# Two fused layers on one core: another order for layer 1's block maxima

## The chip, the cores and the metric

One core of one Trainium2 chip runs the whole program; there is one launch and no other core takes part. The metric is device time of that core in microseconds (us), the median of the runs shown. TensorE (PE in the profile, with its weight loads as PEld), VectorE (DVE), ScalarE (ACT), GpSimd (POOL) and the DMA queue of SyncE (SP) each work through their own list of instructions in order and meet at semaphores.

## The reference, cut to what matters

The input has 4 batches of 2048 rows of 256 numbers. Layer 0 is a gated recurrence plus an attention over 4 chosen heads. Layer 1, where the change lies, is a causal attention with 16 heads of 16 numbers plus a channel mix. All is in float32.

```python
def _L1_attn_ref(x, W_q, b_q, W_k, b_k, W_v, b_v, W_o, b_o):
    ...
    scores = jnp.einsum('bhid,bhjd->bhij', Qh, Kh) / jnp.sqrt(jnp.asarray(Dh, dtype=x.dtype))
    causal = jnp.tril(jnp.ones((S, S), dtype=x.dtype))
    scores = scores * causal - NEG_BIG * (1.0 - causal)
    attn = jax.nn.softmax(scores, axis=-1)
    vals = jnp.einsum('bhij,bhjd->bhid', attn, Vh)
    ...
    return vals @ W_o + b_o
...
x = x + _L1_attn_ref(xn, ...) + _L1_ffn_ref(xn, ...)
```

The softmax needs, for each query and head, the largest score over the keys that the mask leaves.

## The kernel before

**Groups, blocks, units.** Layer 1 takes its 16 heads in 4 groups `g` of 4. The 4 heads of a group lie in four strips of 32 partitions, so that four matmuls with 32 rows each can run side by side. Queries and keys are cut into 4 blocks of 512 (`q` for queries, `kc` for keys) and each block into 4 tiles of 128 rows (`t`).

**Maxima.** A `Maxima(q, t, kc)` unit computes the scores of one tile of 128 queries against one block of keys for the four heads: four matmuls (L767), each into one PSUM bank, and a VectorE reduction of each. A unit with `kc < q` is full: 512 columns, reduced by a plain TENSOR_REDUCE (L773). A unit with `kc == q` lies on the diagonal and is masked: it has only (t + 1) * 128 columns, and its reduction (L770) adds the mask. Block `q` has 4(q + 1) units, four of them masked, with 128, 256, 384 and 512 columns. When all units of a block are done, `turn` reduces and transposes the maxima (L832, L835) and sends them by four DMAs on SP into a spare row of the query tile. From then on the maximum is subtracted by the score matmul itself.

**Weights.** A `Weights(q, t)` unit takes one tile of 128 keys against a block of 512 queries: four matmuls (L792), four exponentials on ScalarE (L794), for the four diagonal tiles a mask on GpSimd (L797), later four matmuls with the values (`weigh`, L803), a copy out of PSUM by ScalarE (L809) and an addition on GpSimd (L810). Its width is 512, or on the diagonal 512, 384, 256 and 128 in turn. Block `q` has 4q + 4 of these, so a group has 40 units of each kind.

**How they are paired.** The loop of `layer1` makes one step of one Weights unit `w` and one Maxima unit `m`, and `Leading` runs the maxima 20 units ahead of the weights (the first 20 of a batch are done while layer 0's attention ends and layer 1 opens):

```python
for h in range(0, 4, 2):
    w.scores(h)
    w.scores(h + 1)
    if m is not None:
        m.scores(2 - h)
        m.scores(3 - h)
if before is not None:
    weigh(before)
```

A step so issues eight score matmuls in two rounds of four, two strips for `w` and two for `m`, and then the four value matmuls of the step before. Each takes the next of the 8 PSUM banks (`own_bank`): nine banks are asked for per step, so a bank comes round again in the next step and must have been emptied by then. Everything is issued in program order on each engine (`in_order`).

Steps are numbered 0 to 39 in a group here. The Maxima unit in step n is the 20th after: steps 4 to 19 carry block 3 of the same group, steps 20 to 23 block 0 of the next group, 24 to 31 block 1, 32 to 39 and the 0 to 3 that follow block 2. In the last group of a batch no maxima are left from step 20 on.

Of the kernel before, what the change touches and what calls it, by code (L numbers as in the profile page):

```python
# [18 lines left out]
P = 128  # L19
QB = 512  # L20
EPS = 1e-5
MASKED = -1e30


# [48 lines left out]
def two_layers(ctx: ExitStack, tc: tile.TileContext, x, Wa, Wx, ba, bx, Lam,  # L73
# [8 lines left out]
    NT = T // P  # L82
    NQ = T // QB
    NH, NA, DH = 16, 4, 64
    NG, DH1 = 4, 16
    SC0 = 1.0 / math.sqrt(DH)
    LN8 = math.log(8.0)
# [40 lines left out]
    def rows_of(both, n, count):  # L128
# [13 lines left out]
    POOL.memset(cmask, 0.0)  # L142
    POOL.affine_select(out=cmask[:, QB - P:QB], in_=cmask[:, QB - P:QB], compare_op=ALU.is_ge, fill=MASKED,
                       base=0, pattern=[[-1, P]], channel_multiplier=1)
    eps_c = const.tile([P, 1], FP, tag="eps", name="eps_c")
    POOL.memset(eps_c, EPS)
    quarter_c = const.tile([P, 1], FP, tag="quarter", name="quarter_c")
# [607 lines left out]
    class Maxima:  # L755
# [9 lines left out]
        def scores(self, h):  # L765
# [3 lines left out]
            if self.own:  # L769
                DVE.tensor_tensor_reduce(out=s[:, 0:n], in0=s[:, 0:n], in1=cmask[:, QB - n:QB], scale=1.0,  # L770
                                         scalar=2 * MASKED, op0=ALU.add, op1=ALU.max, accum_out=self.mx[:, h, :])
            else:
# [39 lines left out]
    class Leading:  # L812
# [6 lines left out]
        def all(self):  # L819
            for g in range(NG):  # L820
                for q in range(NQ):
                    mx = sm.tile([P, 4, 4, q + 1], FP, tag="mx1", name=f"mx1_{self.b}_{g}_{q}",
                                 padded_shape=[P, 4, 4, NQ])
                    for t in range(4):
                        for kc in range(q + 1):
                            yield Maxima(q, t, kc, *self.qk[g], mx)
                    self.turn(g, q, mx)

        def turn(self, g, q, mx):
# [272 lines left out]
```

## Time and profile before

| What | Before |
|---|---|
| Median of 3 runs | 4263.85 us (4263.78 to 4267.86) |
| Profiled execution, its own time | 4265.95 us |
| Span of that execution | 4264.2 us |
| Mean granted TensorE clock | 0.995 |
| PE busy | 4155.7 us (97%) |
| DVE busy | 3103.7 us (73%) |
| ACT busy | 2809.0 us (66%) |
| POOL busy | 1044.7 us (25%) |
| L767, matmuls of the maxima | 1138.7 us busy, 5120 of them |
| L773, reductions of full units | 951.7 us busy, 1536 of them |
| L770, reductions of masked units | 473.2 us busy, 1024 of them |
| L792, score matmuls of the weights | 1075.4 us busy, 5120 of them |

Each of the 4 batches runs through the same stages in the same order; layer 1's loop is the stretch from 593 to 1084 us in the first of them. Busy time counts an instruction from its start to its end, also where several of one engine overlap, so a PE that is busy need not be working at its full rate.

### The profile page before, as it was taken

The page shows a single profiled execution, that of the slowest core. Times are in us where ns is not written, and L with a number is a line of the kernel's source. Part 1 is how long each engine was busy: PE and PEld are TensorE (multiplying, and loading weights), DVE is VectorE, ACT ScalarE, POOL GpSimd, SP SyncE. Part 2 cuts the span into 40 slices and gives each one's busy share as a digit, 9 for nine tenths or more (in the row PEclk, how much of TensorE's full clock was granted, in tenths as well). Part 3 has the DMA queues.
Part 4 walks back from the last instruction along what each step waited for, and adds up shares of the span by engine and source line. Part 5 has one row for each costly group of instructions (what it writes and reads, how often), then busy time and mean ns, then how long its engine had stood idle before and what let it go on. Part 6 is the DMA issues. An engine that isn't in the chain of part 4 may idle for free.

```text
span 4264.2 us, 86371 instructions
## 1 busy us (share of the span) xinstructions
PE 4155.7 (97%) x32994; PEld 2300.1 (54%) x32994; DVE 3103.7 (73%) x7292; ACT 2809.0 (66%) x6388; POOL 1044.7 (25%) x1322
## 2 busy tenths in 40 slices
PE   6999999999999999999999999999999999999998
PEld 3777643334477764333457776433446777643334
DVE  5777678887577767888757776788856767688882
ACT  3666648886566655888656665588865666568884
POOL 0000015544100002654410000255440000036544
PEclk9999999999999999999999999999999999999999
DMA  3000010100100001110000000011000000101000
GB/s 86 1 11 1 6 19 16 18 26 17 27 1 11 1 6 19 17 37 6 19 24 1 11 1 9 16 17 37 7 19 23 1 11 1 21 6 17 16 7 23
DMA packets 70818, 65.79 MB, mean 15 GB/s; under 512 B 37234, under 2 KB 58628, under 8 KB 68868
## 3 DMA queue, kind: packets, MB, share of 16 engines
q1 hardware_dynamic: 66624, 57.19, 6.1%
q8 instruction: 260, 4.26, 0.4%
q10 hardware_dynamic: 3780, 3.07, 0.2%
q14 instruction: 154, 1.26, 0.1%
HBM read 16.70 MB, written 8.39 MB: 6 GB/s over the span
## 4 chain that ended last, share of the span: by engine, by line
PE 89%; DVE 5%; ACT 3%; issue 1%; POOL 1%; DMA 1%; ACTq 0%; SPq 0%; POOLq 0%; DVEq 0%
PE bank L792 15%; PE bank L767 13%; PE bank L803 12%; PE bank L515 10%; PE bank L493 10%; PE bank L540 10%; PE bank L989 4%; PE bank L698 3%; PE bank L289 3%; PE bank L553 2%; DVE mx L773 1%; PE bank L472 1%; PE bank L455 1%; PE bank L977 1%; DVE mx L497 1%
## 5 line engine op out<-in xcount | busy, mean ns | idle before, releaser
L794 ACT ACTIVATE p<-bank 128x512 f32<-128x512 f32 (+3 forms) x2560 | 1183.3, 540 | 299.7 <-PE bank L792 194.9
L767 PE MATMUL bank<-k,q 32*128 32x512 f32 (+3 forms) x5120 | 1138.7, 569 | 1.7
L773 DVE TENSOR_REDUCE mx<-bank 128x1 f32<-128x512 f32 x1536 | 951.7, 682 | 238.1 <-PE bank L767 235.1
L792 PE MATMUL bank<-q,k 32*128 32x512 f32 (+3 forms) x5120 | 1075.4, 557 | 0.0
L507 ACT ACTIVATE p<-bank,nm 128x512 f32<-128x512 f32 x1024 | 689.5, 685 | 568.1 <-DVE nm L501 568.0
L810 POOL TENSOR_TENSOR o<-o,w 128x512 f32<-128x512 f32 (+3 forms) x576 | 627.3, 1089 | 796.6 <-ACT w L809 795.0
L792 PEld LDWEIGHTS bank<-q,k 32*128 32x128 f32 x5120 | 422.9, 184 | 547.1 <-ACT p L794 407.0
L497 DVE TENSOR_REDUCE mx<-bank 128x1 f32<-128x512 f32 x1024 | 645.8, 683 | 93.7 <-PE bank L493 93.1
L803 PE MATMUL bank<-p,v 128*17 128x512 f32 (+3 forms) x5120 | 602.9, 535 | 21.7 <-ACT p L794 14.3
L521 DVE COPY pT<-bank 128x512 f32<-128x512 f32 x512 | 352.7, 691 | 294.1 <-PE bank L515 277.9
L770 DVE CUSTOM_DVE_ANT_0 bank<-bank,cmask 128x128 f32<-128x128 f32 (+3 forms) x1024 | 473.2, 522 | 111.5 <-PE bank L767 56.3
L540 PEld LDWEIGHTS bank<-pT,v 128*64 128x64 f32 x8192 | 441.9, 137 | 193.2 <-issue 193.2
L493 PE MATMUL bank<-k,q 64*128 64x512 f32 x2048 | 542.8, 610 | 1.1 <-ACT p L507 0.3
L515 PE MATMUL bank<-ident,p 128*128 128x128 f32 x4096 | 492.1, 275 | 19.9 <-ACT p L507 19.7
L540 PE MATMUL bank<-pT,v 128*64 128x128 f32 x8192 | 503.7, 276 | 0.0
L767 PEld LDWEIGHTS bank<-k,q 32*128 32x128 f32 x5120 | 430.8, 184 | 129.5 <-DVE mx L773 42.4
L515 PEld LDWEIGHTS bank<-ident,p 128*128 128x128 f32 x4096 | 445.3, 141 | 71.1 <-ACT p L507 29.4
L706 POOL MEMSET q<- 128x2048 f32 x16 | 28.9, 1805 | 1655.1 <-PE bank L540 1655.1
L809 ACT COPY w<-bank 128x512 f32<-128x512 f32 (+3 forms) x576 | 305.4, 530 | 107.8 <-PE bank L803 85.2
L521 ACT COPY pT<-bank 128x512 f32<-128x512 f32 x512 | 293.4, 600 | 61.6 <-PE bank L515 59.7
L803 PEld LDWEIGHTS bank<-p,v 128*17 128x17 f32 x5120 | 88.8, 95 | 441.0 <-ACT p L794 236.6
L493 PEld LDWEIGHTS bank<-k,q 64*128 64x128 f32 x2048 | 211.5, 188 | 171.1 <-issue 84.3
(164 smaller groups left out, 3350.6 us busy)
## 6 DMA issues: line engine op xcount, KB each, us to landing
x<-in_L_attn_x_dram SPq DMA_DIRECT2D x20, 512.0 KB
q<-q SPq DMA_DIRECT2D x64, 128.0 KB
vals<-o SPq DMA_DIRECT2D x256, 32.0 KB
out_dram<-x SPq DMA_DIRECT2D x32, 256.0 KB
q<-qp SPq DMA_DIRECT2D x48, 128.0 KB
k<-kp SPq DMA_DIRECT2D x48, 128.0 KB
q<-nmT SPq DMA_DIRECT2D x256, 2.0 KB
q<-qp SPq DMA_DIRECT2D x64, 32.0 KB
```

What stands on the lines that cost most here:

```text
L493: PE.matmul(self.s[j][i], lhsT=self.qT[i][half_, self.t * P:(self.t + 1) * P], rhs=self.kT[half_, j * QB:(j + 1) * QB], start=True, stop=True)
L497: DVE.tensor_reduce(self.mx[:, n:n + 1], self.s[j][i], AX.X, ALU.max)
L507: ACT.activation(self.p[j][:, i, :], self.s[j][i], AF.Exp, bias=nm, accum_out=self.sums[:, n:n + 1])
L515: PE.transpose(self.tr[j][i][:, n * P:(n + 1) * P], self.p[j][:, i, n * P:(n + 1) * P], ident)
L521: copy(self.pT[:, n0:n0 + 4, :], self.tr[j][i].rearrange("p (n q) -> p n q", q=P))
L540: PE.matmul(acc[i * DH:(i + 1) * DH, 0:P], lhsT=self.v[h][:, N * j + n, self.k * DH:(self.k + 1) * DH], rhs=tile_.pT[:, 8 * h + N * j + n, ...
L767: PE.matmul(s[:, 0:n], lhsT=self.qT[strip(h), self.qs], rhs=self.kT[strip(h), self.ks], start=True, stop=True)
L773: DVE.tensor_reduce(self.mx[:, h, :], s[:, 0:n], AX.X, ALU.max)
L792: PE.matmul(s[:, c0:QB], lhsT=self.kT[strip(h), self.ks], rhs=self.qT[strip(h), self.q0 + c0:self.q0 + QB], start=True, stop=True)
L794: ACT.activation(p[:, h % 2, c0:QB], s[:, c0:QB], AF.Exp, scale=SC1)
L803: PE.matmul(acc[32 * h:32 * h + DH1 + 1, c0:QB], lhsT=self.v[h], rhs=self.p[h // 2][:, h % 2, c0:QB], start=True, stop=True)
L810: POOL.tensor_tensor(self.o[:, c0:QB], self.o[:, c0:QB], w[:, c0:QB], ALU.add)
```

## The change

The order of the Maxima units within a block is read from a table. An entry is a tile digit and a key block digit: "23" is tile 2 against key block 3. The units of a block, their matmuls and reductions, the tile of maxima they write and the moment of `turn` stay what they are.

```diff
+MAXIMA = ("30 20 10 00", "30 11 10 00 20 21 31 01", "31 30 20 11 22 21 12 10 00 32 01 02",
+          "02 23 31 21 00 30 03 13 12 33 32 22 10 01 11 20")
...
+    assert NQ == len(MAXIMA)
...
-                    for t in range(4):
-                        for kc in range(q + 1):
-                            yield Maxima(q, t, kc, *self.qk[g], mx)
+                    for unit in MAXIMA[q].split():
+                        yield Maxima(q, int(unit[0]), int(unit[1]), *self.qk[g], mx)
```

The pairs that result in the steps of a group, with the width of the Weights unit, and for the Maxima unit f for a full one and the number of columns for a masked one:

```
steps     weights           maxima before                    maxima after
0 to 3    512 384 256 128   384 f f 512                      f 512 f 128
4 to 7    512 (all)         f f f 128                        f 384 f f
8 to 11   512 384 256 128   f f f 256                        f f 128 256
12 to 19  512 (all)         f f f 384 f f f 512              f 512 f f f f f f
20 to 23  512 384 256 128   128 256 384 512                  512 384 256 128
24 to 31  512 (all)         f 128 f 256 f 384 f 512          f 256 f f f 384 512 128
32 to 35  512 (all)         f f 128 f                        f f f f
36 to 39  512 384 256 128   f 256 f f                        384 f 256 f
```

## The prediction

> **What bounds the kernel now.** I read the page first, then the timeline of one group, then busy time by stretches of its steps.
>
> ```profile
> PE 4155.7 (97%) x32994; PEld 2300.1 (54%) x32994; DVE 3103.7 (73%) x7292; ACT 2809.0 (66%) x6388; POOL 1044.7 (25%) x1322
> ...
> PE 89%; DVE 5%; ACT 3%; issue 1%; POOL 1%; DMA 1%; ACTq 0%; SPq 0%; POOLq 0%; DVEq 0%
> ```
>
> By the engine totals and the chain of waits PE is the bound, and the change takes no work from it. Whether it works at its full rate must be seen in the steps. Two steps with a full unit on both sides, third group of the first batch:
>
> ```profile
> 869.19 0.19 PEld L792 LDWEIGHTS bank<-q,k 32*128 32x128 f32 x2 [0.85 <-ACT p L794]
> ...
> 869.48 0.62 ACT L809 COPY w<-bank 128x512 f32<-128x512 f32 x1
> ...
> 870.35 2.06 ACT L794 ACTIVATE p<-bank 128x512 f32<-128x512 f32 x4 [0.25 <-PE bank L767]
> 870.43 2.48 DVE L773 TENSOR_REDUCE mx<-bank 128x1 f32<-128x512 f32 x4 [0.62 <-PE bank L767]
> ...
> 871.20 1.05 PE L803 MATMUL bank<-p,v 128*17 128x512 f32 x8
> ```
>
> A step runs from one such L792 load to the next. Most full steps take 2.91 us: two rounds of scores and one of values, 0.97 us each (1.9 ns a column). This one takes 3.00, because it follows a masked unit. ACT needs 2.06 + 0.62, DVE 2.4 (four reductions, one every 0.60 to 0.62 us). So PE is full only where both units are full. Where `w` is 512 wide and `m` is masked with 128 to 384 columns, the step falls only to 2.79 (ACT's), and the next full one takes 3.00: a short `m` beside a full `w` saves 0.03 us. Next, the same group by steps 0-5, 6-7, 8-13, 14-19, 20-24, 25-35, 36-39:
>
> ```profile
> 824.22:841.20 16.98, 16.96 (x149) 7.32 (x145) 15.75 (x37) 12.26 (x30) 8.24 (x14) 1.00 0.10 17
> 841.20:846.90 5.70, 5.38 (x53) 2.08 (x49) 4.64 (x15) 4.76 (x10) 4.25 (x3) 1.00 0.40 72
> 846.90:863.48 16.58, 16.48 (x148) 6.63 (x144) 13.67 (x28) 13.22 (x31) 8.94 (x14) 1.00 0.74 170
> 863.48:881.15 17.67, 17.65 (x148) 6.37 (x144) 14.19 (x30) 15.27 (x30) 6.34 (x5) 1.00 0.04 9
> 881.15:894.28 13.13, 12.97 (x124) 6.12 (x121) 10.35 (x42) 10.23 (x26) 8.51 (x13) 1.00 0.01 3
> 894.28:926.45 32.17, 31.60 (x269) 11.75 (x265) 24.57 (x68) 28.21 (x56) 11.88 (x10) 1.00 0.03 6
> 926.45:937.24 10.79, 10.78 (x100) 4.38 (x96) 8.84 (x21) 8.13 (x21) 7.83 (x12) 1.00 0.01 2
> ```
>
> Columns: length, then busy PE, PEld, DVE, ACT, POOL. PE shows busy throughout, yet its columns in these 113.0 us (3 x 17408 x 1.9 ns) are 99 us. The 14 us between are lost where widths don't match; two such places:
>
> ```profile
> 856.47 0.30 PEld L767 LDWEIGHTS bank<-k,q 32*128 32x128 f32 x4 [0.29 <-DVE mx L773]
> ...
> 884.97 0.43 DVE L770 CUSTOM_DVE_ANT_0 bank<-bank,cmask 128x256 f32<-128x256 f32 x1 [1.30 <-PE bank L792]
> ```
>
> In step 11 (`w` 128) PE waits for a bank that VectorE, late from the full unit in step 10 (`w` 256), has not emptied. In step 21 VectorE stands idle 1.30 us, since its units are short while `w` is long; in step 23 (`w` 128, `m` 512) it is the last instead.
>
> **The change part by part.** It adds and removes nothing: same matmuls, reductions, DMAs, each in its old place in its engine's list, with another width. `turn` with its SP DMAs comes after the same unit count, and the steps between it and its first reader stay four or more (about 9 us against 2.5 us for its DMAs). What moves is which widths meet. Per group, masked units beside a 512 `w` go from 10 to 8, and beside narrow ones the small `m` now meets the small `w`.
>
> For each step I take the largest of: PE, (w + m + w of the step before) x 1.9 ns; DVE, four reductions at 0.60 us full, and 0.65, 0.51, 0.38, 0.25 masked by width (spacing in the timeline), plus 0.65 for `turn`; ACT, 2.79 for a 512 `w` behind another, else four exponentials (2.06 at 512, 0.89 at 128) and the copy (0.60 to 0.30); POOL, 0.82 for the diagonal mask and 1.27, 1.00, 0.72 or 0.45 for the addition. The ratio of measured to this sum is carried over.
>
> Steps 20 to 24. Before 2.79 + 2.18 + 2.06 + 2.60 + 3.05 = 12.68, measured 13.13 (x1.035). After 2.91 + 2.43 + 1.82 + 1.54 + 2.51 = 11.21 (PE, PE, POOL, POOL, DVE; step 23 leaves VectorE room for part of `turn`), x1.035 = 11.60. Gain 1.5.
>
> Steps 36 to 39 and 0 to 5. Before 2.91 + 2.18 + 2.40 + 2.40 + 2.36 + 2.67 + 2.40 + 2.60 + 3.05 + 2.91 = 25.88, measured 10.79 + 16.98 = 27.77 (x1.073). After 2.79 + 2.67 + 1.82 + 2.40 + 2.40 + 2.67 + 2.40 + 1.54 + 2.51 + 2.79 = 23.99, x1.073 = 25.74: gain 2.0. I take 1.7, as in short steps the delay from a matmul to the freed bank weighs more.
>
> Steps 8 to 13. Before 2.91 + 2.67 + 2.40 + 1.54 + 2.40 + 2.91 = 14.83, measured 16.58. After, step 10 falls to 1.82 (POOL): ratio alone gives 0.65. Following the banks by hand (VectorE no longer late in step 11) gives 1.2. I take 0.9. In the second group POOL also adds a bias in each of these steps (L923, 0.73 us): 0.3 there.
>
> Costs. Full units moved beside a 512 `w`: 0.1 a group. In the last group the mix makes VectorE the bound in steps 14 to 17 (4.98 us busy of 5.00 in the stretch 987 to 992), and step 15 gets a full unit for a 384: 0.4 a batch. In the 20 leading units, 256 more columns (0.43 us of PE, 1.1 of DVE), and the first unit is 512 wide, not 128: its VectorE work of 2.6 us, not 1.0, stands ahead of two copies of layer 0's attention (L521). VectorE idled 4.44 us before it, and the four units' sum is the same. Nothing to 3.8 us; I take 1.2.
>
> Per batch: 3 x 1.5 + 3 x 1.7 + 0.5 (the first group's own steps 0 to 5, half covered by layer 1's opening) + 3 x 0.9 + 0.3 - 4 x 0.1 - 0.4 - 1.2 = 11.1. Four batches: 44 us. The profiled execution took 4265.95 us, 1.75 outside its span, and is 2.1 above the median; the change lies within the span, so I take it off the median: 4263.85 - 44.4 = 4219.5.
>
> **Two rules against the trace.** The row PE 97% says that at most 3% is to be had; taken as the bound, the group could give 113.02 - 111.82 = 1.2 us, 14 to 16 us in all. The Trainium skill, "Perfetto Trace Analysis", Identifying the Most-Contended Engine, says that matmul busy time is a bad measure because matmuls are pipelined, and to look at weight loads: 54% here. I follow it, and the 99 us of columns with it. Against the change speaks "TensorEngine Tiling (Array Packing)", PSUM Bottleneck: tiling speeds up TensorE but not the emptying of PSUM, which may then bind. As a rule for totals it gives no gain, since DVE and ACT empty the same columns as before. The rows say DVE 92.0 and ACT 92.1 of 113.0 us: neither is full over a group, but each is last in some steps, and that is what the pairing changes. I go by the rows, and keep the rule for the rivals.
>
> **The rivals.** (a) GpSimd takes over in the short steps. Its mask and addition are in order, and `weigh` waits for the mask. If steps 3, 10, 22, 23, 38 stay near 2.3 us (step 11 now: 2.23), steps 20 to 24 gain 0.5, 36 to 5 gain 1.0, 8 to 13 0.4: 1.5 + 3.0 + 0.3 + 1.4 - 2.0 = 4.2 a batch, 17 us, 4247. For: 8.51 us busy of 13.13 in steps 20 to 24. Against: 4.6 us of room.
> (b) No change: the narrow steps gain 3 to 6 a batch, little more than in (a), and the lead takes its full 3.8, so that the costs are 4.6: 4258 to 4270. For: the two copies that VectorE makes late feed layer 0's last value matmuls. Against: its 4.44 us of idle time just before.
> (c) Slower. A wide pair makes VectorE late, and the step behind it pays at the bank ring: step 1 now takes 3.17 where its PE sum is 2.67. If step 21 behind the new 512 pair takes 3.17 and 22 and 23 stay at 2.44 and 2.36, 20 to 24 is 2.91 + 3.17 + 2.44 + 2.36 + 2.97 = 13.85, 0.7 more; 36 to 5 lose 0.2, 8 to 13 gain 0.2: 2.1 + 0.6 - 0.8 + 2.0 = 3.9 a batch, 4279. It decides if step 21 takes over 3 us and step 23 stays over 2.2. Against: step 22 and 23 need less of VectorE than they last, so lateness dies out there.
> (d) That the change doesn't do what it says: it does not keep masked units apart (block 0 has only such, block 1 ends with three in a row). My sum does not rest on that.
>
> **How the numbers follow.** My forecast 0.64 (4198 to 4240; the lower end has the hand-followed gains of 1.75, 2.0 and 1.2 and no costs, 65 us); (a) 0.18; (b) 0.09; (c) 0.09. About 0.2%, 8.5 us, is what a measurement of this kernel tells from no change. Faster (below 4255.3) 0.82: forecast and (a); same 0.09: (b); slower 0.09: (c). The range, 4197 to 4258, takes in (a) and ends where (b) begins.
>
> **What would show it.** Right: per group, steps 20 to 24 near 11.6 us, 36 to 5 near 26, 8 to 13 near 15.6, steps 24 to 35 unchanged, the waits of L767 for L773 and L770 (42.4 and 19.6 us) smaller, granted clock still 0.995. POOL: L803 waiting for L797 grows from 38.4 us. Wrong: step 21 over 3 us or 23 over 2.2; a lead of more than 61.86 + 2 us from the first L767 to the first L792; or 24 to 35 longer by over 0.5.

## The result, and the profile after

| What | Before | After |
|---|---|---|
| Median | 4264.70 us (the three runs of before and one more) | 4233.02 us (4 runs, 4232.47 to 4234.65) |
| Ratio, 95% interval | | 0.9926 (0.9910 to 0.9941) |
| Span of the profiled execution | 4264.2 us | 4232.9 us |

The changed kernel is 31.7 us faster: 0.74%, with an interval of 0.6 to 0.9%. The forecast was 44 us. Line numbers after the change are 5 higher around the loop (L767 is now L772, L792 is L797, L803 is L808) and 4 higher further down; in experiments that add a line they are one higher still.

The page of the changed kernel, the engine totals and the chain of waits by engine:

```profile
PE 4129.7 (98%) x32994; PEld 2283.5 (54%) x32994; DVE 3107.5 (73%) x7292; ACT 2797.4 (66%) x6388; POOL 1044.9 (25%) x1322
...
PE 90%; DVE 5%; ACT 2%; issue 1%; POOL 1%; DMA 1%; ACTq 0%; SPq 0%; POOLq 0%; DVEq 0%
```

These totals do not tell what happened: as many instructions, the same shares to a point, and PE "busy" for 26 us less with the same matmuls. The steps tell it. Busy time of the third group of the first batch in the same seven stretches as before (steps 0-5, 6-7, 8-13, 14-19, 20-24, 25-35, 36-39; length, then busy PE, PEld, DVE, ACT, POOL):

```profile
819.62:835.84 16.22, 16.11 (x148) 7.34 (x144) 14.96 (x41) 12.16 (x30) 8.42 (x15) 1.00 0.12 19
835.84:841.66 5.82, 5.82 (x52) 1.98 (x48) 5.05 (x11) 4.91 (x11) 4.24 (x3) 1.00 0.56 94
841.66:857.29 15.63, 15.62 (x148) 6.56 (x144) 13.09 (x37) 12.94 (x31) 8.93 (x14) 1.00 0.70 170
857.29:874.76 17.47, 17.47 (x148) 5.74 (x144) 14.71 (x25) 15.05 (x30) 6.34 (x5) 1.00 0.04 9
874.76:886.87 12.11, 12.11 (x125) 5.22 (x121) 10.30 (x40) 9.51 (x25) 8.52 (x13) 1.00 0.01 3
886.87:918.96 32.09, 31.75 (x268) 11.43 (x265) 25.96 (x64) 28.42 (x57) 11.88 (x10) 1.00 0.03 6
918.96:929.30 10.34, 10.32 (x100) 4.70 (x97) 8.26 (x24) 8.15 (x21) 7.63 (x12) 1.00 0.01 2
```

The group takes 109.7 us where it took 113.0, and the gain lies in the three places with narrow weights: 13.13 to 12.11, 27.77 to 26.56 (steps 36 to 39 with 0 to 5), 16.58 to 15.63. The stretches with wide weights alone stay within 0.2 us. The same from the timeline of all four batches (lengths in us, batch 1 being the first; "last" is the fourth group, which has no maxima from step 20 on; the lead is the stretch ahead of the loop in which the first 20 Maxima units run):

| Stretch | Before | After | Forecast of the gain | Gain |
|---|---|---|---|---|
| Steps 20 to 24, groups 1 to 3 | 13.13 | 12.10 (once 12.36) | 1.5 | 1.03 |
| Steps 36 to 39 and 0 to 5 that follow | 27.75 | 26.56 | 1.7 | 1.19 |
| Steps 0 to 5, group 1 | 19.7 to 21.9 | 18.27 | 0.5 | 1.5 to 3.7 |
| Steps 8 to 13, groups 1 and 3 | 16.58 | 15.63 | 0.9 | 0.95 |
| Steps 8 to 13, group 2 | 17.1 to 17.4 | 17.07 (batch 1: 18.83, part of it at half clock, see the last section) | 0.3 | 0.0 (batch 1: -1.4) |
| Steps 8 to 13, last group | 16.73 | 16.39 | 0.9 | 0.34 |
| Steps 14 to 19, last group | 21.02 | 21.55 | -0.4 | -0.53 |
| Lead, first L767 to first L792 | 61.86 | 64.52 | -1.2 | -2.66 |

### The profile page after: what moved, and what is told of

Its sections match the earlier page's. It is cut to its first block, busy times and chain, and to the rows that moved or that the text cites. A ratio compares the mean times of both kernels' runs of the same rounds, so it can differ in the third digit from the quotient of the medians.

```text
span 4232.9 us, 86387 instructions
## 1 busy us (share of the span) xinstructions
PE 4129.7 (98%) x32994; PEld 2283.5 (54%) x32994; DVE 3107.5 (73%) x7292; ACT 2797.4 (66%) x6388; POOL 1044.9 (25%) x1322
## 4 chain that ended last, share of the span: by engine, by line
PE 90%; DVE 5%; ACT 2%; issue 1%; POOL 1%; DMA 1%; ACTq 0%; SPq 0%; POOLq 0%; DVEq 0%
PE bank L797 15%; PE bank L772 13%; PE bank L808 12%; PE bank L520 11%; PE bank L498 10%; PE bank L545 10%; PE bank L993 4%; PE bank L703 3%; PE bank L294 3%; PE bank L558 2%; DVE mx L778 1%; PE bank L477 1%; PE bank L460 1%; PE bank L981 1%; DVE mx L502 1%; ACT p L512 1%
## 5 line engine op out<-in xcount | busy, mean ns | idle before, releaser
L772 PE MATMUL bank<-k,q 32*128 32x512 f32 (+3 forms) x5120 | 1139.1, 564 | 3.2 <-DVE mx L778 1.3
L797 PE MATMUL bank<-q,k 32*128 32x512 f32 (+3 forms) x5120 | 1089.6, 555 | 0.0
L797 PEld LDWEIGHTS bank<-q,k 32*128 32x128 f32 x5120 | 418.4, 184 | 533.7 <-ACT p L799 445.5
L808 PE MATMUL bank<-p,v 128*17 128x512 f32 (+3 forms) x5120 | 602.9, 534 | 16.6 <-POOL p L802 11.7
L775 DVE CUSTOM_DVE_ANT_0 bank<-bank,cmask 128x512 f32<-128x512 f32 (+3 forms) x1024 | 473.3, 521 | 75.0 <-PE bank L772 56.4
L520 PE MATMUL bank<-ident,p 128*128 128x128 f32 x4096 | 492.3, 275 | 19.9 <-ACT p L512 19.7
L772 PEld LDWEIGHTS bank<-k,q 32*128 32x128 f32 x5120 | 426.7, 183 | 136.7 <-DVE mx L778 34.5
L808 PEld LDWEIGHTS bank<-p,v 128*17 128x17 f32 x5120 | 89.7, 95 | 431.1 <-ACT p L799 235.8
```

Of the source, the lines that this page charges most:

```text
L520: PE.transpose(self.tr[j][i][:, n * P:(n + 1) * P], self.p[j][:, i, n * P:(n + 1) * P], ident)
L772: PE.matmul(s[:, 0:n], lhsT=self.qT[strip(h), self.qs], rhs=self.kT[strip(h), self.ks], start=True, stop=True)
L797: PE.matmul(s[:, c0:QB], lhsT=self.kT[strip(h), self.ks], rhs=self.qT[strip(h), self.q0 + c0:self.q0 + QB], start=True, stop=True)
L808: PE.matmul(acc[32 * h:32 * h + DH1 + 1, c0:QB], lhsT=self.v[h], rhs=self.p[h // 2][:, h % 2, c0:QB], start=True, stop=True)
```

## The experiments

All ratios are against runs of the kernel before on the same chip. In every table the digits have the meaning of the change.

**One block at a time.** Do the rows of the table work alone, and do they add up?

```diff
-MAXIMA = ("30 20 10 00", "30 11 10 00 20 21 31 01", "31 30 20 11 22 21 12 10 00 32 01 02",
-          "02 23 31 21 00 30 03 13 12 33 32 22 10 01 11 20")
+MAXIMA = ("30 20 10 00", "00 01 10 11 20 21 30 31", "00 01 02 10 11 12 20 21 22 30 31 32",
+          "00 01 02 03 10 11 12 13 20 21 22 23 30 31 32 33")
```

This is block 0 alone; the next two keep the row of block 2 or of block 3 in the same way and put the other three in the order of before.

> Table with the new order in block 0 alone, the other blocks in the old order. Theory (widths: what counts is which width meets which in a step): steps 20 to 24 fall from 13.13 to 12.1 us in the 12 groups that have maxima there, the lead grows from 61.86 to about 63.2 (the 1.3 us by which block 1's first unit starts later in the lead), all other stretches stay: 4264.7 - 12.4 + 5.3 = about 4257.6. Rival (spacing: what counts is that masked units lie apart): block 0 has only masked units, in either order, so nothing is gained in steps 20 to 24 and the time is that of before or, with the lead, 4270.

Measured: 4257.84 us, 0.9984 (0.9978 to 0.9991). Steps 20 to 24 take 12.17 to 12.56, the lead 63.18.

> New order in block 2 alone. Theory (widths): steps 36 to 39 go from 10.80 to 10.35, steps 0 to 5 of the second to fourth group from 16.95 to about 16.3, the lead gets about 1.5 us longer, the first group's steps 0 to 5 about as much shorter: 12 x 1.1 = 13 us, so about 4252; less (down to 4245) if the half-clock stretch at the start of layer 1's loop stays away as well. Rival (the rows of the table work only together): well under half of that, 4259 or more.

Measured: 4247.62 us, 0.9961 (0.9947 to 0.9975). Steps 36 to 39 take 10.34, steps 0 to 5 16.43, the lead 63.40, and the first group's steps 0 to 5 18.42 in all batches: the half-clock stretches of the kernel before, worth 5.2 us (see below), stayed away in this profile.

> New order in block 3 alone. Theory (widths): steps 8 to 13 go from 16.58 to about 15.6 in the first and third group, from 16.73 to 16.4 in the last, and stay near 17.1 in the second, where GpSimd is the bound; steps 6 to 7 cost 0.12 each group and steps 14 to 17 of the last group 0.5: 4 x (2 x 0.95 + 0.35 - 0.5 - 0.5) = 5 us, about 4260; step 4 to 5 of 6.1 stays. Rival (rows together): no gain, 4265 or more.

Measured: 4257.38 us, 0.9980 (0.9974 to 0.9987). Steps 8 to 13 take 15.63 in groups 1 and 3 and 16.38 in the last; steps 0 to 5 of the later groups fall by 0.2 as well, 2.6 us in all, about what separates this run from the 4260 that were expected.

The three gains, 7.1, 17.3 and 7.5 us, add to 31.8; the whole table gained 31.7. That it fits to 0.1 us is luck, since the intervals of the single gains are some 3 to 6 us wide on either side; but the rows act in their own stretches, little is left for block 1's row (whose steps all have wide weights), and the idea that only the whole table works falls.

**The same places, other widths.** Is it that masked units lie apart, or which width meets which?

```diff
-MAXIMA = ("30 20 10 00", "30 11 10 00 20 21 31 01", "31 30 20 11 22 21 12 10 00 32 01 02",
-          "02 23 31 21 00 30 03 13 12 33 32 22 10 01 11 20")
+MAXIMA = ("00 10 20 30", "30 11 10 00 20 21 31 01", "31 30 20 11 02 21 32 10 00 12 01 22",
+          "02 03 31 21 00 30 33 23 12 13 32 22 10 01 11 20")
```

> Masked units in the very places of the new table, but with their widths exchanged inside blocks 2 and 3 so that wide masked units meet narrow weights and the narrow ones meet 512 wide weights (block 0 in the old, ascending order; block 1 as in the new table). Theory (widths): steps 20 to 24 are back at 13.1, step 10 at about 2.6 and steps 38 and 3 at 2.6 to 2.7, so nearly all of the gain is gone: 4255 to 4268. Rival (spacing): only block 0's part is lost, 12 us: 4233 + 12 - 5 (lead) = about 4240.

Measured: 4261.11 us, 0.9990 (0.9981 to 0.9999). The third group of the first batch, steps 8-13, 20-24 and 36-39:

```profile
844.42:860.98 16.56, 16.43 (x149) 6.71 (x145) 14.72 (x38) 12.69 (x31) 8.95 (x14) 1.00 0.73 168
...
878.45:891.58 13.13, 12.81 (x124) 6.05 (x121) 10.18 (x40) 10.23 (x26) 8.52 (x13) 1.00 0.01 3
923.68:935.01 11.33, 11.01 (x100) 4.47 (x97) 8.78 (x25) 8.26 (x21) 7.82 (x12) 1.00 0.01 2
```

The first two are back at the lengths of before, 16.58 and 13.13, though every masked unit of block 3 stands where the new table has one. Steps 36 to 39 are longer than in either kernel, but steps 0 to 5 after them take 15.89: together 27.2, against 27.75 before and 26.56 after, so there about half of the gain stayed, which I had not expected. The first groups ran partly at half clock in all four batches of this profile, so the stretches say more than the time. The spacing theory (4240, and only steps 20 to 24 back at their old length) falls: the gain of steps 8 to 13 and 20 to 24 comes from the widths, and half of that in steps 36 to 5; why the other half stayed there is open.

**The lead.** Block 0 of a batch's first group in the old order:

```diff
-                    for unit in MAXIMA[q].split():
+                    for unit in ("00 10 20 30" if g == q == 0 else MAXIMA[q]).split():
```

> The changed kernel, but the very first block of a batch (group 0, block 0, done in the lead) in the old order. Theory (in the lead VectorE's wide first unit delays the two copies of layer 0's attention behind it): the lead falls from 64.52 to about 63.2, the loop stays, 4233 - 5.3 = about 4228. Rival (the lead is longer because of the wider units of block 2 alone): 4233, lead 64.5.

Measured: 4227.08 us, 0.9910 (0.9893 to 0.9926), and the lead is 63.19. VectorE and PE in the lead of the changed kernel, then VectorE in this one:

```profile
533.85 1.28 DVE L526 COPY pT<-bank 128x512 f32<-128x512 f32 x2
...
534.67 0.30 PEld L772 LDWEIGHTS bank<-k,q 32*128 32x128 f32 x4 [0.33 <-DVE pT L526]
```

```profile
531.47 1.28 DVE L526 COPY pT<-bank 128x512 f32<-128x512 f32 x2
```

With the 512 wide unit first, the two copies of layer 0's attention start 3.7 us after that unit's matmuls (530.12 in the timeline), and PE waits for the banks that they empty; with the 128 wide one first they start after about 1.5. Half of the lead's 2.66 us is this. The other half fits block 2's row (61.86 to 63.40 when it alone was changed).

**The group in which nothing was gained.** The bias additions on GpSimd moved out of steps 0 to 15:

```diff
+WIDE = (*range(14, 20), *range(24, 34))
...
-            if g == 1 and n % 40 < NT:
-                xs = rows_of(x1, n % 40, 1)[:, 0, :]
+            if g == 1 and n % 40 in WIDE:
+                xs = rows_of(x1, WIDE.index(n % 40), 1)[:, 0, :]
```

> The changed kernel, but the 16 GpSimd additions of the output bias to x in the second group are moved from its steps 0 to 15 to its steps 14 to 19 and 24 to 33, all with 512 wide weights. Theory (in the second group GpSimd is the bound of steps 10 to 12): steps 8 to 13 of that group fall from 17.07 (18.83 in the first batch) to 15.63, 4 x 1.44 to 7.6 in sum: about 4226, and no half-clock stretch near 740 us. Rival (VectorE's late banks are the bound there as in the other groups): no change, 4233.

Measured: 4229.78 us, 0.9919 (0.9902 to 0.9935); steps 8 to 13 of group 2 fall to 16.39, half of what was expected, and to just what the last group takes. So something else holds both groups. (In this profile three of the first groups also ran their steps 0 to 5 partly at half clock, which cost 3.2 us.) GpSimd's work for step 10 in this kernel, done late, when PE is already in step 11:

```profile
736.29 1.26 POOL L892 TENSOR_TENSOR vals<-vals,spread 128x512 f32<-128x512 f32 x1
737.51 0.76 POOL L803 TENSOR_SCALAR_AFFINE_SELECT p<-p 128x256 f32<-128x256 f32 x2
```

A multiplication by the inverse sums, which only the second and fourth group have, stands ahead of the masks. In the last group of the changed kernel PE's value matmuls of step 11 wait for those masks:

```profile
961.00 0.12 PEld L808 LDWEIGHTS bank<-p,v 128*17 128x17 f32 x4 [0.75 <-POOL p L802]
```

**That multiplication put off.**

```diff
-            later.put(12, multiply)
+            later.put(18 if q == 0 else 12, multiply)
```

> The changed kernel, but GpSimd's multiplication by the softmax's inverse sums for query block 0 (L891, due in step 9 of the second and the last group, seen in step 10) is put off by six slots, to step 12. Theory (in those groups this multiplication stands ahead of the masks for which step 11's value matmuls wait): steps 8 to 13 fall from 16.39 to 15.63 in the last group and by up to 0.75 in the second, where the bias additions still stand: 4 x 0.75 to 8 x 0.75, about 4228 (4226 to 4231). Rival (these groups are slower there for another reason): 4233 and 16.39 unchanged.

Measured: 4232.68 us, 0.9926 (0.9910 to 0.9943). The stretch did what was expected, 15.63 in the last group and 15.84 in the second (16.15 in the first batch), but the time stayed: step 14 of the last group went from 4.13 to 5.60 and that of the second from 2.91 to 3.25. GpSimd and VectorE in the last group:

```profile
963.11 1.42 POOL L891 TENSOR_TENSOR vals<-vals,spread 128x512 f32<-128x512 f32 x1 [0.43 <-DVE spread L890]
964.47 0.12 POOL L965 MEMSET xk<- 128x1 f32 x2
...
964.60 0.75 DVE L968 SCALAR_TENSOR_TENSOR xk<-xT,cols,xk 128x512 f32<-128x512 f32 x1 [1.21 <-POOL xk L965]
```

The multiplication now stands ahead of a small memset (L965) that the channel mix on VectorE waits for. The cause was right, but of the 9.4 us that steps 8 to 13 gained over the four batches, steps 14 to 19 of the same groups gave 7.2 back, and half-clock stretches, in the first group of all four batches of this profile, cost another 4.9.

**What limits the matched narrow steps.**

```diff
-                ACT.copy(w[:, c0:QB], acc[:, c0:QB])
-                POOL.tensor_tensor(self.o[:, c0:QB], self.o[:, c0:QB], w[:, c0:QB], ALU.add)
+                k0, other = (QB - P, cmask) if self.own else (c0, w)
+                ACT.copy(w[:, k0:QB], acc[:, k0:QB])
+                POOL.tensor_tensor(self.o[:, c0:QB], self.o[:, c0:QB], other[:, c0:QB], ALU.add)
```

> The changed kernel, but ScalarE's copy of a diagonal unit's weighed values out of PSUM takes the last 128 columns alone, and GpSimd's addition for it, as wide as before, adds a constant tile in place of that copy: this part of the output is left out. Theory (in matched narrow steps the last score matmul waits for the bank that this copy empties): step 22 falls from 2.22 to about 1.93, step 23 from 1.69 to about 1.5, step 10 by 0.3, 12.10 to about 11.6 in steps 20 to 24, about 4217 in all. Rival (GpSimd's mask and addition bound those steps, which stay as wide): steps 22 and 23 stay, 4230 to 4236.

Measured: 4220.60 us, 0.9896 (0.9879 to 0.9912). Step 22 fell from 2.22 to 2.09, step 23 from 1.69 to 1.56, step 39 from 2.33 to 2.12 (step 0 behind it rose from 2.78 to 2.99); step 10 stays at 2.09, but step 11 behind it fell from 1.89 to 1.68. By the stretches, the profiled execution would have been some 3.8 us shorter still without half-clock stretches in the first groups of all four batches. First, step 22 of the changed kernel, then of this one:

```profile
880.59 0.19 PEld L797 LDWEIGHTS bank<-q,k 32*128 32x128 f32 x2 [0.85 <-ACT p L799]
...
880.79 0.59 ACT L814 COPY w<-bank 128x512 f32<-128x512 f32 x1 [0.46 <-PE bank L808]
...
881.42 0.29 PEld L772 LDWEIGHTS bank<-k,q 32*128 32x128 f32 x2
...
882.05 0.13 PEld L808 LDWEIGHTS bank<-p,v 128*17 128x17 f32 x8 [0.33 <-issue]
```

```profile
878.81 0.27 ACT L815 COPY w<-bank 128x128 f32<-128x128 f32 x1 [0.46 <-PE bank L808]
...
879.41 1.21 ACT L799 ACTIVATE p<-bank 128x256 f32<-128x256 f32 x4 [0.33 <-PE bank L772]
...
879.90 0.16 PEld L808 LDWEIGHTS bank<-p,v 128*17 128x17 f32 x8 [0.49 <-issue]
```

In the changed kernel the last score matmul loads at 881.42, 0.04 us after the copy has emptied the bank (880.79 + 0.59); it is the eighth request after that copy's own bank, so it gets the same one. With the short copy that load comes earlier, and the value matmuls start at 879.90, 1.29 us into the step, not at 1.46. So the copy was a cap, and less than half of the 0.32 us by which it shrank here (0.59 to 0.27) came through. The next cap I read from the trace but did not test: the value matmuls take the bank of the step's own first scores, whose exponential, first of the four at 879.41, has just ended. GpSimd's work was as wide as ever, so it was not the bound of steps 22 and 23. What holds step 10 at 2.09 is open.

**Better versions.** First the old order in the lead and the moved bias additions together, with block 2's masked units in other widths:

```diff
-"31 30 20 11 22 21 12 10 00 32 01 02"
+"31 30 20 11 32 21 02 10 00 12 01 22"
```

> Old order for the first block of a batch, the bias additions moved, and in block 2 the masked widths placed anew (512 in step 36, 128 in step 38, 256 in step 1, 384 in step 3). Theory: the gains of the first two add to 4221; block 2's new widths bring steps 0 to 5 from 16.22 to about 15.9 (as in the exchanged table) with steps 36 to 39 unchanged near 10.4: about 4217. Rival (the three share one slack): 4226 or more.

Measured: 4222.70 us, 0.9902 (0.9885 to 0.9918). Between the two: the lead and the bias gave their part, block 2's new widths nothing (steps 0 to 5 16.23, 36 to 39 10.45). The 15.9 of the exchanged table had been for the most part time moved across the boundary: its step 39 took 2.89 and its step 0 2.36, where the changed kernel has 2.33 and 2.78. Then, with the table's own block 2 and the multiplication put off:

> The new table unchanged, the first block of a batch in the old order, the bias additions moved and the multiplication put off. Theory: the gains add: lead 63.2, steps 8 to 13 at 15.63 in all four groups: 4 x (1.33 + 1.44 + 0.75) = 14 us below the changed kernel, about 4218 (4216 to 4221). Rival (the combination before, 4222.7, is the floor of these edits): 4222 or more.

Measured: 4223.65 us, 0.9905 (0.9888 to 0.9921): 15.63 in steps 8 to 13 of all groups but one, and steps 14 to 19 of the last group at 23.0, as when the multiplication alone was put off. Last, it is put off in the second group only:

```diff
+            later.put(18 if q == 0 and g == 1 else 12, multiply)
```

> As the combination before, but the multiplication is put off in the second group alone; in the last group it stays where it was. Theory (put off in the last group, it stands ahead of the GpSimd memset for which VectorE's mix waits in step 14): step 14 of the last group is back at 4.13 from 5.6 while its steps 8 to 13 are back at 16.39, 4 x (1.47 - 0.76) = 2.8 us less: about 4221. Rival (step 14's loss has another cause): 4223 or more.

Measured: 4220.76 us, 0.9893 (0.9877 to 0.9910). This is the best whole kernel here, 12 us below the changed one. The intervals of the three combinations overlap; their order rests on the stretches, which moved as expected: steps 8 to 13 of the second group take 15.63 and step 14 of the last 4.13.

## Why the prediction was right, and where its sizes were off

**The bound and the mechanism: right.** The row "PE 97%" was not a cap. After the change it reads 98%, in a kernel that is 31 us shorter with the same matmuls; the third group gained 3.3 us where that row left 1.2. Weight loads read 54% both times, so they did not show the gain either; the count of columns did, 99 us of work in 113.0 and now in 109.7. The rule on emptying PSUM, taken for totals, would have given no gain: VectorE's and ScalarE's work in the group is the same (92.0 and 92.3, 92.1 and 91.1 us), and the exchanged widths show that most of the gain is in the pairing.

**Steps 8 to 13: right in two groups, wrong in two.** 0.95 for the forecast 0.9 in the first and third. The step that failed is "3 x 0.9 + 0.3": the sum gave GpSimd the masks, the additions and in group 2 the bias, and left out the multiplication L887, which stood in the listing of the groups all along with 32 instructions of 1271 ns. Put off, it left 15.84 and 15.63 in the two groups. With it the second group gained nothing and the last 0.34. That costs the forecast about 0.9 us a batch (0.3 + 0.56). It is rival (a)'s mechanism, in two groups.

**Steps 20 to 24: mechanism right, size off.** 1.03 and not 1.5. Step 21 was put at 2.43 x 1.035 and took 2.85 to 2.92; step 22 at 1.88 and took 2.22; step 24 was put at 2.60 and took 2.36. In step 21 the trace has what rival (c) said, in a smaller size:

```profile
878.57 0.14 DVE L775 DVE_READ_ACCUMULATOR2_ANT mx<- 128x1 f32 x1
878.76 0.30 PEld L772 LDWEIGHTS bank<-k,q 32*128 32x128 f32 x4
```

VectorE ends the 512 wide unit of step 20 at 878.71, and only then PE loads for step 21's last two scores, 1.0 us into the step. The largest of four engine sums leaves such hand-overs out, and carrying over a ratio measured on mismatched steps did not put them back. The short copy showed the size of one of them: 0.13 us in each of steps 22 and 23.

**Steps 36 to 5: 1.19 and not 1.7.** Steps 37, 0, 1 and 3 took 3.00, 2.78, 3.14 and 2.07 where the sum with its ratio had 2.86, 2.58, 2.86 and 1.65. In step 3 the trace has the same kind of hand-over:

```profile
827.92 1.28 DVE L778 TENSOR_REDUCE mx<-bank 128x1 f32<-128x512 f32 x2
...
829.25 0.30 PEld L772 LDWEIGHTS bank<-k,q 32*128 32x128 f32 x4 [0.30 <-DVE mx L778]
```

VectorE ends the full unit of step 2 at 829.20, 1.0 us into step 3, and PE's loads for the last two scores have waited 0.30 us for it. That steps 37, 0 and 1 lost time in the same way is not shown. I had taken 0.3 off the sum's 2.0 for such delays; that was too little.

**The lead: wrong by more than the line drawn for it.** 2.66 a batch, not 1.2; the prediction itself named more than 2 as a sign against it. Both causes it named are there: the wide first unit, 1.33 by the experiment, and block 2's wider units, about 1.5 when they alone were changed. It counted the "4.44 us of idle time just before" as cover, but that idle time lies before the unit's matmuls have run and can hide nothing after them.

**The first group's steps 0 to 5: a gain not foreseen.** 0.5 was forecast, and 11 us came in four batches. Of these 5.2 are not the pairing: in three batches of the profiled execution before, this stretch took 20.5 to 21.9 with the clock at half, in the fourth 19.72 without. Against 19.72 the gain is 1.45 a batch. The later groups gained 0.73 in the same steps, so about half of it is the pairing. The other half may be that block 2's wider masked units now lie in the lead: with that row alone changed the lead grew by 1.54 while these steps fell from 19.7 to 18.42. No run separates the two.

The sum: 44.4 - 5.8 (lead) - 5.6 (steps 20 to 24) - 6.1 (36 to 5) - 3.6 (GpSimd's groups) + 9.0 (first group's steps) = 32.3, against 31.3 between the two spans. Batch 1's half-clock stretch in group 2 (1.8) is not in it, and small terms give 0.8 back. That the total came as near to the forecast as it did is in part luck: the 9.0 us that nobody had foreseen, 5.2 of them a matter of the clock, stand against 21 us by which its other terms were too favourable.

**What was to show it.** Steps 24 to 35 unchanged: yes for 25 to 35, 32.16 and 32.09 (step 24, counted with 20 to 23, fell from 2.97 to 2.36). The waits of PE's loads for the maxima's banks: 42.4 + 19.6 before, 34.5 + 20.4 after, smaller but not gone. The waits of PE's loads for GpSimd's mask did not grow over the whole kernel (38.4 to 34.4, and with those of its matmuls 44.6 to 46.1), so by that sign alone its part in two groups would have been missed.

## What to carry to other kernels

Where two streams of work of changing width share one loop, look at the steps and not at the engine totals: pair narrow with narrow, since a short partner beside a long one saves next to nothing (0.03 us here), and exchange the widths in place to see whether it is that. The largest of the engines' sums gives the sign and the place, but in short steps it left out the hand-over of a buffer from one engine to the next. The stretches with short steps fell short by a quarter of the forecast gain (5.6 + 6.1 of 44.4 us); the traces show hand-overs in several of these steps, not that they are all of it. So count who takes a freed bank next. List all that stands in an in-order queue at the step in question, work that comes there only in some groups included, and price what the new order puts at the start of a pipeline by itself: here the lead cost 2.66 us a batch, more than twice the 1.2 put down for it, and half of that was the first unit's width.

## What the runs showed that was not expected

TensorE's clock was at half for 3.4 or 6.8 us at a time at the start of layer 1's loop, in three of the four batches before, in none after, and in none to four in the experiments' profiles. (All profiles have more such stretches outside that loop.) In the kernel before, then the one such stretch inside the loop after, in batch 1's second group (the last but two of a row's numbers is the granted clock):

```profile
596.30:603.10 6.80, 6.80 (x31) 3.88 (x28) 5.47 (x14) 3.15 (x6) 1.22 (x3) 0.50 0.00 0
```

```profile
740.00:743.40 3.40, 3.40 (x20) 1.22 (x16) 0.78 (x2) 1.18 (x3) 3.37 (x6) 0.50 0.00 0
```

The mean over the span reads 0.995 in both kernels and hides it. In the 3.4 us ahead of the second stretch PE was busy for 2.06 us, but ahead of the first for the whole of 3.40, so idle time in the PE row does not tell when it comes. Where it came in the kernel before, steps 0 to 5 of the first group were 0.8 to 2.2 us longer. The Trainium skill, "TensorE: Matmul & The Clock Gate", Part 1, says that the clock is set by activity in a window of about 3.4 us that runs free of the kernel; the lengths here, one and two such windows, agree. About 3.4 us of the 31.3 between the two profiled spans is this (5.2 before less 1.8 after). What decides whether it comes was not settled: at the start of the loop it was absent in five of the profiles with the table's block 2 and present in three (the moved bias, the short copy, the multiplication put off alone).
